# Attention, then two quantised convolutions: one projection of both pairs of heads per image, and fifteen images of the first convolution in DRAM

## The chip, the cores and the metric

The kernel runs on one core of a Trainium2 chip. The metric is the device time of one execution in microseconds; the median of the runs is quoted. An engine is named by the short names of the profile: PE is TensorE, DVE is VectorE, ACT is ScalarE, POOL is GpSimd, SP is SyncE (which only issues DMAs here).

## The reference

Two layers on x of shape (16, 128, 32, 32) in fp32: 16 images, 128 channels, N = 32 x 32 = 1024 positions. The first is self-attention with 4 heads of 128 channels each, an output projection and a residual. The second is two 3x3 convolutions with activations and weights quantised to 4 bits, a batch norm over all 16 images after each, and a residual.

```python
def _L0_conv_ref(x, w_qkv, b_qkv, w_out, b_out):
    qkv = jnp.einsum('bchw,oc->bohw', x, w_qkv) + b_qkv[None, :, None, None]
    ...
    scores = jnp.einsum('bnc,bcm->bnm', q, k) * c ** (-0.5)
    attn = jax.nn.softmax(scores, axis=-1)
    out = jnp.einsum('bnm,bmc->bnc', attn, v)
    ...
    out = jnp.einsum('bchw,oc->bohw', out, w_out) + b_out[None, :, None, None]
    return out + x

def _L1_conv_ref(x, w1, w2, gamma1, beta1, gamma2, beta2):
    identity = x
    out = act_quant(x)
    out = conv3x3(out, weight_quant(w1))
    out = batchnorm(out, gamma1, beta1)
    out = act_quant(out)
    out = conv3x3(out, weight_quant(w2))
    out = batchnorm(out, gamma2, beta2)
    return out + identity
```

The batch norm is the seam of the program: no image can be quantised for the second convolution before the first convolution of the last image is done.

## The kernel before, in words

The weights are folded first, so that the scores of a head are x times u with u = A x (tiles `psu`, `u`), and the values of every head are x itself; the output matrix B of a head holds both its value and its output weights.

**The attention, 63 of 64 heads in one pattern.** A head is 4 steps (NK = 4). A step computes four score tiles of 128 keys by 512 queries (`scores`, tiles `pss`, in three PSUM banks), turns each into exponentials on ACT (L585), and lets DVE form sums and differences of them (`mix`, L570 to L574). Half a step later `attend` (L597) multiplies them with the values by a Strassen-like scheme: a 2x2 block product in seven products and not eight, in four PSUM banks `psa` a0 to a3. TensorE is used as two independent halves of 64 columns, called lanes here (`LANES`, TOP and BOTTOM in the output's partitions); each product goes to one lane. Seven is odd, so one lane has one product more than the other in a step; `attend` alternates which.

At a head's end `evacuate` (L622) copies the four banks to SBUF on ACT, `combine` (L631) decodes them, `sum_up` and `normalise` (L698) divide by the sums of the exponentials. Two heads make a pair: `normalise` writes the two halves of head h into `z`, a tile of 7 blocks, and after the second head `mix` fills in the other three blocks of the scheme.

**The output projection.** `project_out` (L738) multiplies `z` of a pair with `wb_sb` by the same scheme, one PSUM bank after the other, all in the single bank `ps_m` ("mm") which `project_u` uses too. It is called for both pairs of an image, so there are 8 such banks per image. After each bank, ACT copies it out (L760 to L773). `gather_out` (L775) adds the pieces; the second pair's result is added to the first's in `accs[b]`, then bias and residual, and it is stored to `x1d`. The last image uses `project_plain` (L720) for its heads 0 and 1, and a separate tail (L873 writes its last sums).

**What sets the order.** On TensorE `product` (L400) ties every matmul behind the one issued before it. Everything else of the attention is placed by hand: `at(step, half, fn)` (L1018 on) puts a function behind the scores (half 0) or behind the products (half 1) of a step. Within that, the order on ACT, DVE, POOL and SP comes from the scheduler of the framework and from explicit `issue_after`; each engine then takes its instructions in that order.

**The two convolutions.** The first convolution of image b runs between the later heads' steps (tiles `psw`). Its output y stays in SBUF for images 0, 1 and 15; for `AWAY = range(2, B - 1)`, images 2 to 14, it goes to `y1d` in DRAM. After the last image, `bn_params(0)` gives scale and bias (L339), three loads bring `back` in groups of 2, 3 and 8 images (L1172 to L1174), `res` loads the residuals (L1179), and the second convolution runs image by image (L1238 to L1252): `quantize2` (L1181: ACT at L1189 from `y` or `back`, DVE at L1190 and L1194 into a padded tile), then nine taps (`conv`, tiles `psc`), or for `FILTERED` = 3, 5, 7, 9, 11, 13 a cheaper scheme (`filtered_conv`, L1209, tiles `psf`) with input rows from DVE and POOL (L1205) and four combinations on DVE (L1226 to L1229). DVE takes statistics at L298 (L292 for image 15), `gather` at L272 sums them, and after the second `bn_params` the last loop (L1255) writes the outputs.

Of the kernel before, what the change touches and what calls it, by code (L numbers as in the profile page):

```python
# [9 lines left out]
F32 = mybir.dt.float32  # L10
BF16 = mybir.dt.bfloat16
AF = mybir.ActivationFunctionType
ALU = mybir.AluOpType
# [3 lines left out]
NH = 4  # L17
# [176 lines left out]
def fast_path(  # L194
# [17 lines left out]
    P = 128  # L212
# [29 lines left out]
    AWAY = range(2, B - 1)  # L242
# [125 lines left out]
    with ExitStack() as ph:  # L368
# [5 lines left out]
        zp = pool("z", 1)  # L374
# [7 lines left out]
        accp = pool("acc", 2)  # L382
# [239 lines left out]
        def evacuate(g):  # L622
            evs[g] = [evp.tile([P, HALF], F32, tag=f"s{i}", name=f"ev_{g}_{i}") for i in range(4)]
            for to, ps in zip(evs[g], psa.pop(g)):
                nc.scalar.copy(to, ps)  # L625
# [72 lines left out]
        def normalise(g):  # L698
# [11 lines left out]
            if h % 2 == 0:  # L710
                zs[b] = zp.tile([P, 7, HALF], F32, tag="z", name=f"z_{b}_{h}")
            z = zs[b]
            for m in range(NHF):
                nc.vector.tensor_tensor(  # L714
                    z[:, 2 * (h % 2) + 1 - m], av[:, ts(m, HALF)], rb[:, ts(m, HALF)], ALU.mult
                )
            if h % 2:
                mix(z)

        def project_plain(g, m):  # L720
# [3 lines left out]
            ps = ps_m.tile([P, HALF], F32, tag="mm", name=f"pso_{g}_{m}")  # L724
            halves(ps, lambda t: bt_sb[:, h, LANES[t]], av[:, ts(m, HALF)])
            if h == 0:
                if m == 0:
                    accs[b] = accp.tile([P, N], F32, tag="acc", name=f"acc_{b}")
                nc.scalar.copy(accs[b][:, ts(m, HALF)], ps)
            else:  # L730
                half = accs[b][:, ts(m, HALF)]
                own = pjp.tile([P, HALF], F32, tag=("sa", "sb")[m], name=f"own_{m}")
                nc.scalar.copy(own, ps)
                nc.vector.tensor_tensor(half, half, own, ALU.add)
# [3 lines left out]
        def project_out(b, pair, bank):  # L738


            z = zs[b]
            four = [
                [(0, A11, B11)],
                [(1, A22, T4), (0, A12, B21)],
                [(1, S2, T2), (0, S4, B22)],
                [(1, S1, T1)],
            ]
            four[3 * pair].append((1 - pair, S3, T3))
            ps = ps_m.tile([P, HALF], F32, tag="mm", name=f"pso_{b}_{pair}_{bank}")
            for t, weight, head in four[bank]:  # L750
                product(ps[LANES[t]], wb_sb[:, weight, pair], z[:, head])
            if (b, pair) not in pjs:
                names = ("sa", "sb", "s3", "sd", "y", "s2")
                pjs[b, pair] = [
                    pjp.tile([P, HALF], F32, tag=n, name=f"{n}_{b}_{pair}") for n in names
                ]
            sa, sb, s3, sd, y, s2 = pjs[b, pair]
            if bank == 0:
                if pair == 0:
                    nc.scalar.copy(sa, ps)  # L760
                    nc.scalar.copy(y[BOTTOM], ps[BOTTOM])
                else:
                    nc.scalar.copy(sa[TOP], ps[TOP])  # L763
# [5 lines left out]
            else:  # L769
                nc.scalar.copy(sd[BOTTOM], ps[BOTTOM])  # L770
                nc.scalar.copy(sd[TOP], ps[BOTTOM])
                if pair == 1:
                    nc.scalar.copy(y[BOTTOM], ps[TOP])  # L773

        def gather_out(b, pair, part):  # L775

            sa, sb, s3, sd, y, s2 = pjs[b, pair]
# [8 lines left out]
            else:  # L786
                pjs.pop((b, pair))
                for half, first, second in ((1, y, sd), (0, sa, sb)):
                    if pair == 0:
                        if half:  # L790
                            accs[b] = accp.tile([P, N], F32, tag="acc", name=f"acc_{b}")
                        to = accs[b][:, ts(half, HALF)]
                        nc.vector.tensor_tensor(to, first, second, ALU.add)
                    else:
                        to = accs[b][:, ts(half, HALF)]
                        nc.vector.tensor_tensor(first, first, second, ALU.add)
# [744 lines left out]
```

## Time and profile before

| what | value |
|---|---|
| median of 3 runs | 2015.97 us (2015.92 to 2017.56) |
| profiled execution | 2017.06 us |
| span in its profile | 2015.2 us |
| granted TensorE clock, mean | 0.993 |
| one image of the attention | 118.8 us |
| last `psa` matmul of the attention ends | 1918.07 us |
| batch norm 1's bias done (L339) | 1925.25 us |
| first matmul of the second convolution | 1926.51 us |
| last matmul | about 1982.6 us |

The span is what the profiler saw; the execution's own time has 1.86 us around it. A row of the page's group list has the line, engine and operation, the tiles written and read, the shape, the number of instructions, then busy time and mean duration, and last the idle time just before these instructions with what ended it. A row of the timeline has start, duration, engine, line, operation, tiles and count. Durations of matmuls overlap: one is 0.59 us long while the next has started, so a busy TensorE may still be late.

The shares by slice of the span show an even attention, and after it the hand-over and the second stage in the last two or three of the 40 slices:

```profile
PE   9999999999999999999999999999999999999993
...
DVE  5886879778687877868787786888878698786887
```

### The profile page before, as it was taken

How to read it: one execution, taken by the hardware profiler on the slowest of the kernel's cores; microseconds unless marked ns; L12 is line 12 of the kernel's file. 1: busy time of each engine (PE TensorE's matmuls, PEld its weight loads, DVE VectorE, ACT ScalarE, POOL GpSimd, SP SyncE). 2: the span in 40 equal slices, each digit the busy share in tenths (PEclk: the TensorE clock that was granted, in tenths of full speed). 3: DMA queues.
4: the chain of work that ended last, by engine and by line, in shares of the span. 5: the costliest groups of instructions: out<-in, count | busy, mean ns of one | idle time of the engine just before them, and what ended most of it. 6: DMA issues, size and time to landing. Idle time of an engine off the chain costs nothing. (4 is left out here: it accounts for less than half of the span.)

```text
span 2015.2 us, 26154 instructions
## 1 busy us (share of the span) xinstructions
PE 1978.1 (98%) x9636; PEld 1072.0 (53%) x9637; DVE 1605.5 (80%) x2793; ACT 1267.6 (63%) x2148; POOL 182.9 (9%) x218
## 2 busy tenths in 40 slices
PE   9999999999999999999999999999999999999993
PEld 4455465554646555464555546555554655556541
DVE  5886879778687877868787786888878698786887
ACT  4566666666656656765665666666666566666575
POOL 1100010010000000000101000000100100000020
PEclk9999999999999999999999999999999999999997
DMA  4334333333343343334333333433333333433174
GB/s 122 85 81 97 72 80 90 84 90 88 86 95 82 97 92 84 94 74 100 85 99 84 90 89 74 110 79 94 84 95 95 73 97 86 91 84 79 42 314 168
DMA packets 55672, 191.70 MB, mean 95 GB/s; under 512 B 6128, under 2 KB 6512, under 8 KB 55536
## 3 DMA queue, kind: packets, MB, share of 16 engines
q0 software_dynamic: 27216, 99.10, 26.1%
q1 hardware_dynamic: 25200, 81.08, 10.4%
q10 hardware_dynamic: 3120, 9.77, 1.6%
q8 instruction: 77, 1.26, 0.3%
q14 instruction: 59, 0.48, 0.1%
HBM read 34.22 MB, written 23.59 MB: 29 GB/s over the span
## 5 line engine op out<-in xcount | busy, mean ns | idle before, releaser
L403 PE MATMUL pss<-u,x 128*64 128x512 f32 (+1 forms) x4128 | 1045.1, 590 | 0.0
L403 PE MATMUL psa<-e,xt 128*64 128x512 f32 x3472 | 907.5, 592 | 0.0
L585 ACT ACTIVATE e<-pss 128x512 f32<-128x512 f32 x1008 | 589.6, 597 | 299.0 <-PE pss L403 293.4
L403 PEld LDWEIGHTS pss<-u,x 128*64 128x64 f32 x4128 | 474.4, 137 | 402.7 <-issue 225.6
L403 PEld LDWEIGHTS psa<-e,xt 128*64 128x64 f32 x3472 | 418.9, 137 | 335.8 <-issue 203.4
L571 DVE TENSOR_TENSOR e<-e 128x1024 f32<-128x1024 f32 x252 | 307.6, 1221 | 16.2 <-ACT e L585 11.6
L595 POOL DMA_DIRECT2D es<-e x189 | 163.3, 864 | 1690.8 <-DVE e L574 1391.2
L570 DVE TENSOR_TENSOR e<-e 128x512 f32<-128x512 f32 x252 | 171.2, 679 | 148.9 <-ACT e L585 148.5
L574 DVE TENSOR_TENSOR e<-e 128x512 f32<-128x512 f32 x252 | 173.3, 688 | 14.2 <-DVE e L571 0.5
L625 ACT COPY ev<-psa 128x512 f32<-128x512 f32 x252 | 137.1, 591 | 73.7 <-PE psa L403 72.0
L403 PE MATMUL psu<-x,at_sb 128*64 128x512 f32 x512 | 180.4, 592 | 0.0
L403 PE MATMUL pso<-z,wb_sb 128*64 128x512 f32 x420 | 166.2, 592 | 0.0
L714 DVE TENSOR_TENSOR z<-av,rb 128x512 f32<-128x512 f32 x120 | 78.5, 684 | 51.1 <-PE pso L403 51.1
L534 ACT ACTIVATE u<-psu,au_sb 128x512 f32<-128x512 f32 x127 | 87.4, 688 | 16.9 <-PE psu L403 15.0
L779 DVE TENSOR_TENSOR y<-sa,s 64x512 f32<-64x512 f32 x30 | 20.5, 684 | 92.1 <-ACT sa L763 46.7
L403 PEld LDWEIGHTS psu<-x,at_sb 128*64 128x64 f32 x512 | 65.5, 137 | 47.0 <-issue 22.8
L655 DVE TRANSPOSE_TENSOR_REDUCE part<-es 128x32 f32<-128x1024 f32 (+1 forms) x65 | 79.3, 1220 | 4.9 <-DMA es<-e 4.8
L695 DVE STREAM_TRANSPOSE rb<-sums 128x1024 f32<-128x1024 f32 (+1 forms) x66 | 79.8, 1209 | 1.6
L403 PEld LDWEIGHTS pso<-z,wb_sb 128*64 128x64 f32 x420 | 54.2, 137 | 45.0 <-issue 23.3
L645 ACT COPY ev<-y 64x512 f32<-64x512 f32 x63 | 38.8, 615 | 61.9 <-DVE y L643 61.9
L765 ACT COPY sb<-pso 128x512 f32<-128x512 f32 x30 | 17.6, 586 | 72.0 <-PE pso L403 72.0
L403 PE MATMUL psw<-rows,filters 128*64 128x256 bf16 x540 | 60.2, 278 | 0.0
(197 smaller groups left out, 1476.1 us busy)
## 6 DMA issues: line engine op xcount, KB each, us to landing
es<-e POOLq DMA_DIRECT2D x189, 512.0 KB, 4.5
es<-e SPq DMA_DIRECT2D x63, 512.0 KB, 2.9
xt<-in_xturned_dram SPq DMA_DIRECT2D x32, 256.0 KB, 3.4
x_dram<-acc SPq DMA_DIRECT2D x16, 512.0 KB, 4.5
x<-in_x_dram ACTq DMA_DIRECT2D x15, 512.0 KB, 4.8
res<-x_dram SPq DMA_DIRECT2D x1, 7680.0 KB, 35.7
y_dram<-y SPq DMA_DIRECT2D x13, 512.0 KB, 2.6
out_dram<-back SPq DMA_DIRECT2D x10, 512.0 KB, 3.1
```

What stands on the lines that cost most here:

```text
L403: done = nc.tensor.matmul(out_, lhsT=lhsT, rhs=rhs, start=start, stop=stop)
L534: copied = nc.scalar.activation(dst, ps, AF.Identity, bias=au_sb[:, h : h + 1])
L570: nc.vector.tensor_tensor(e[:, T3], e[:, B12], e[:, B22], ALU.add)
L571: nc.vector.tensor_tensor(e[:, T1 : T2 + 1 : T2 - T1], e[:, B12 : B11 + 1], e[:, B11 : T3 + 1 : T3 - B11], ALU.subtract)
L574: return nc.vector.tensor_tensor(e[:, T4], e[:, T2], e[:, B21], ALU.add)
L585: exps[:] = [nc.scalar.activation(e[:, 2 * c + 1 - m], ps, AF.Exp).ins]
L595: nc.gpsimd.dma_start(out=sides[g], in_=mine, accum_op=ALU.add)
L625: nc.scalar.copy(to, ps)
L645: nc.scalar.copy(sa[BOTTOM], y[BOTTOM])
L655: nc.vector.tensor_reduce(part, total.rearrange("p (k c) -> p k c", c=Q), AX.X, ALU.add, apply_transpose=True,)
L695: nc.vector.transpose(rb, rinv.unsqueeze(2).to_broadcast([P, n, Q]))
L714: nc.vector.tensor_tensor(z[:, 2 * (h % 2) + 1 - m], av[:, ts(m, HALF)], rb[:, ts(m, HALF)], ALU.mult)
```

## The change

- `project_out` is called once per image and bank, after head 3. For each of four banks both pairs' products go into the same bank: pair 0 starts the sum, pair 1 ends it. The seventh product (S3 times T3) of each pair is cut into two halves of 256 columns, one added into bank 0 on lane 1 (W1), one into bank 3 on lane 0 (W2). The matmuls are issued directly and not through `product`. Banks come in the order 2, 1, 3, 0.
- `gather_out` decodes once per image.
- `evacuate` copies banks 1 and 3; the new `evacuate_rest` copies banks 0 and 2 behind the first and the second exponential of the step after.
- `zs` is kept per pair, so pool `z` has two buffers; pool `acc` has one.
- `normalise` of heads 0 and 2 comes one step earlier, its multiplications behind the step's `mix`; the first `turned_differences` one step later.
- `project_plain` (last image): head 0's result goes into a tile `first`; head 1's first bank is a `ps_s` bank, and its two calls come half a step earlier each.
- `AWAY` is images 0 to 14: their y is stored to DRAM. `y1_dram` has 15 images, and the three loads hold images 0 to 1, 2 to 4, and 5 to 14.

```diff
--- before.py
+++ after.py
@@ -239,7 +239,7 @@
     for n in range(2):
         nc.gpsimd.memset(late[n][:, 0:1], float((B - 1) * N))
 
-    AWAY = range(2, B - 1)
+    AWAY = range(0, B - 1)
     ys = [None if b in AWAY else keep.tile([P, N], F32, name=f"y{b}") for b in range(B)]
     pads = []
     for i in range(NPAD):
@@ -371,7 +371,7 @@
         xp = pool("x", 2)
         up = pool("u", 2)
         xtp = pool("xt", 3)
-        zp = pool("z", 1)
+        zp = pool("z", 2)
         pjp = pool("pj", 1)
         ep = pool("e", 3)
         esp = pool("es", 2)
@@ -379,7 +379,7 @@
         evp = pool("ev", 1)
         smp = pool("small", 4)
         rbp = pool("rb", 1)
-        accp = pool("acc", 2)
+        accp = pool("acc", 1)
         stp = pool("stage", 1)
         ps_s = pool("ps_s", 3, space=PSUM)
         ps_a = pool("ps_a", 1, space=PSUM)
@@ -621,8 +621,14 @@
 
         def evacuate(g):
             evs[g] = [evp.tile([P, HALF], F32, tag=f"s{i}", name=f"ev_{g}_{i}") for i in range(4)]
-            for to, ps in zip(evs[g], psa.pop(g)):
-                nc.scalar.copy(to, ps)
+            for i in (1, 3):
+                nc.scalar.copy(evs[g][i], psa[g][i])
+
+        def evacuate_rest(g):
+            for n, i in enumerate((0, 2)):
+                with tc.issue_after(stepped[n]):
+                    nc.scalar.copy(evs[g][i], psa[g][i])
+            psa.pop(g)
 
 
 
@@ -708,59 +714,64 @@
                 nc.vector.scalar_tensor_tensor(accs[b], accs[b], bo2_sb, xt[b], ALU.add, ALU.add)
                 return
             if h % 2 == 0:
-                zs[b] = zp.tile([P, 7, HALF], F32, tag="z", name=f"z_{b}_{h}")
-            z = zs[b]
+                zs[b, h // 2] = zp.tile([P, 7, HALF], F32, tag="z", name=f"z_{b}_{h}")
+            z = zs[b, h // 2]
             for m in range(NHF):
-                nc.vector.tensor_tensor(
-                    z[:, 2 * (h % 2) + 1 - m], av[:, ts(m, HALF)], rb[:, ts(m, HALF)], ALU.mult
-                )
+                with nullcontext() if h % 2 else tc.issue_after(sums_added[0]):
+                    nc.vector.tensor_tensor(
+                        z[:, 2 * (h % 2) + 1 - m], av[:, ts(m, HALF)], rb[:, ts(m, HALF)], ALU.mult
+                    )
             if h % 2:
                 mix(z)
 
+        W0, W1, W2 = slice(0, HALF), slice(0, HALF // 2), slice(HALF // 2, HALF)
+
         def project_plain(g, m):
 
             b, h = heads[g]
             av = avs[g]
-            ps = ps_m.tile([P, HALF], F32, tag="mm", name=f"pso_{g}_{m}")
+            pool_, tag = (ps_s, "s") if (h, m) == (1, 0) else (ps_m, "mm")
+            ps = pool_.tile([P, HALF], F32, tag=tag, name=f"pso_{g}_{m}")
             halves(ps, lambda t: bt_sb[:, h, LANES[t]], av[:, ts(m, HALF)])
             if h == 0:
                 if m == 0:
+                    avs["first"] = stp.tile([P, N], F32, tag="y", name=f"first_{b}")
+                nc.scalar.copy(avs["first"][:, ts(m, HALF)], ps)
+            else:
+                if m == 0:
                     accs[b] = accp.tile([P, N], F32, tag="acc", name=f"acc_{b}")
-                nc.scalar.copy(accs[b][:, ts(m, HALF)], ps)
-            else:
-                half = accs[b][:, ts(m, HALF)]
                 own = pjp.tile([P, HALF], F32, tag=("sa", "sb")[m], name=f"own_{m}")
                 nc.scalar.copy(own, ps)
-                nc.vector.tensor_tensor(half, half, own, ALU.add)
+                nc.vector.tensor_tensor(accs[b][:, ts(m, HALF)], avs["first"][:, ts(m, HALF)], own, ALU.add)
             if m:
                 avs.pop(g)
 
-        def project_out(b, pair, bank):
-
-
-            z = zs[b]
+        def project_out(b, bank):
+
+
             four = [
-                [(0, A11, B11)],
-                [(1, A22, T4), (0, A12, B21)],
-                [(1, S2, T2), (0, S4, B22)],
-                [(1, S1, T1)],
+                [(0, A11, B11, W0), (1, S3, T3, W1)],
+                [(1, A22, T4, W0), (0, A12, B21, W0)],
+                [(1, S2, T2, W0), (0, S4, B22, W0)],
+                [(1, S1, T1, W0), (0, S3, T3, W2)],
             ]
-            four[3 * pair].append((1 - pair, S3, T3))
-            ps = ps_m.tile([P, HALF], F32, tag="mm", name=f"pso_{b}_{pair}_{bank}")
-            for t, weight, head in four[bank]:
-                product(ps[LANES[t]], wb_sb[:, weight, pair], z[:, head])
-            if (b, pair) not in pjs:
+            ps = ps_m.tile([P, HALF], F32, tag="mm", name=f"pso_{b}_{bank}")
+            for pair in range(2):
+                for t, weight, head, cut in four[bank]:
+                    nc.tensor.matmul(
+                        ps[LANES[t], cut],
+                        wb_sb[:, weight, pair],
+                        zs[b, pair][:, head, cut],
+                        start=(pair == 0),
+                        stop=(pair == 1),
+                    )
+            if b not in pjs:
                 names = ("sa", "sb", "s3", "sd", "y", "s2")
-                pjs[b, pair] = [
-                    pjp.tile([P, HALF], F32, tag=n, name=f"{n}_{b}_{pair}") for n in names
-                ]
-            sa, sb, s3, sd, y, s2 = pjs[b, pair]
+                pjs[b] = [pjp.tile([P, HALF], F32, tag=n, name=f"{n}_{b}") for n in names]
+            sa, sb, s3, sd, y, s2 = pjs[b]
             if bank == 0:
-                if pair == 0:
-                    nc.scalar.copy(sa, ps)
-                    nc.scalar.copy(y[BOTTOM], ps[BOTTOM])
-                else:
-                    nc.scalar.copy(sa[TOP], ps[TOP])
+                nc.scalar.copy(sa[TOP], ps[TOP])
+                nc.scalar.copy(y[BOTTOM, W1], ps[BOTTOM, W1])
             elif bank == 1:
                 nc.scalar.copy(sb, ps)
             elif bank == 2:
@@ -769,12 +780,11 @@
             else:
                 nc.scalar.copy(sd[BOTTOM], ps[BOTTOM])
                 nc.scalar.copy(sd[TOP], ps[BOTTOM])
-                if pair == 1:
-                    nc.scalar.copy(y[BOTTOM], ps[TOP])
-
-        def gather_out(b, pair, part):
-
-            sa, sb, s3, sd, y, s2 = pjs[b, pair]
+                nc.scalar.copy(y[BOTTOM, W2], ps[TOP, W2])
+
+        def gather_out(b, part):
+
+            sa, sb, s3, sd, y, s2 = pjs[b]
             if part == 0:
                 nc.vector.tensor_tensor(y[TOP], sa[TOP], s2[TOP], ALU.add)
             elif part == 1:
@@ -784,21 +794,12 @@
                 with tc.issue_after(stepped[3]):
                     nc.scalar.copy(sa[BOTTOM], y[BOTTOM])
             else:
-                pjs.pop((b, pair))
-                for half, first, second in ((1, y, sd), (0, sa, sb)):
-                    if pair == 0:
-                        if half:
-                            accs[b] = accp.tile([P, N], F32, tag="acc", name=f"acc_{b}")
-                        to = accs[b][:, ts(half, HALF)]
-                        nc.vector.tensor_tensor(to, first, second, ALU.add)
-                    else:
-                        to = accs[b][:, ts(half, HALF)]
-                        nc.vector.tensor_tensor(first, first, second, ALU.add)
-                        nc.vector.tensor_tensor(to, to, first, ALU.add)
-                if pair:
-                    nc.vector.scalar_tensor_tensor(accs[b], accs[b], bo2_sb, xt[b], ALU.add, ALU.add)
-                    nc.sync.dma_start(out=x1d[b], in_=accs[b])
-
+                pjs.pop(b)
+                acc = accs[b] = accp.tile([P, N], F32, tag="acc", name=f"acc_{b}")
+                nc.vector.tensor_tensor(acc[:, HALF:], y, sd, ALU.add)
+                nc.vector.tensor_tensor(acc[:, 0:HALF], sa, sb, ALU.add)
+                nc.vector.scalar_tensor_tensor(acc, acc, bo2_sb, xt[b], ALU.add, ALU.add)
+                nc.sync.dma_start(out=x1d[b], in_=acc)
 
 
         GROUPS = [(0, HALF), (HALF, 3 * N // 4), (3 * N // 4, N)]
@@ -1053,27 +1054,26 @@
             end = (g + 1) * NK
             at(end + 1, 0, sum_up, g)
             at(end, 1, evacuate, g)
+            at(end + 1, 0, evacuate_rest, g)
             at(end + 1, 0, combine, g, 0)
             at(end + 1, 1, combine, g, 1)
             at(end + 2, 0, combine, g, 2)
             if b < B - 1:
-                at(end + (3 if h % 2 else 5), 0, normalise, g)
+                at(end + 4 - h % 2, 0, normalise, g)
             elif g < LAST - 1:
                 at(end + 3, 0, normalise, g)
             else:
                 at(end + 2, 1, normalise, g)
             at(max(g * NK + 1, 2), 0, project_u, g + 1, 0)
             at(max(g * NK + 2, 3), 0, project_u, g + 1, 1)
-            if b < B - 1 and h % 2:
-                pair = h // 2
-                when = ((5, 1), (6, 1), (7, 0), (7, 1))
-                for (step, half), bank in zip(when, ((0, 2, 3, 1), (2, 0, 3, 1))[pair]):
-                    at(end + step, half, project_out, b, pair, bank)
-                at(end + 8, 0, gather_out, b, pair, 0)
-                at(end + 8, 0, gather_out, b, pair, 1)
-                at(end + 9, 0, gather_out, b, pair, 2)
+            if b < B - 1 and h == NH - 1:
+                for bank, (step, half) in ((2, (5, 1)), (1, (6, 1)), (3, (7, 0)), (0, (7, 1))):
+                    at(end + step, half, project_out, b, bank)
+                at(end + 8, 0, gather_out, b, 0)
+                at(end + 8, 0, gather_out, b, 1)
+                at(end + 9, 0, gather_out, b, 2)
             elif b == B - 1 and h < 2:
-                for m, (step, half) in enumerate((((4, 1), (5, 1)), ((5, 0), (5, 1)))[h]):
+                for m, (step, half) in enumerate((((4, 1), (5, 1)), ((4, 1), (5, 0)))[h]):
                     at(end + step, half, project_plain, g, m)
             if h == NH - 1:
                 at(end + 9, 1, lambda b: quantize(b, accs[b], A_LEVELS, 0.0), b)
@@ -1087,7 +1087,7 @@
                     at(end + 9, 1, load, b + 2, nc.scalar)
             if h == 2 and b + 1 < B:
                 at(end - 2, 0, load_turned, b + 1, 0)
-                at(end + 2, 1, turned_differences, b + 1, 0)
+                at(end + 3, 1, turned_differences, b + 1, 0)
                 at(end + 3, 0, load_turned, b + 1, 1)
                 at(end + 6, 1, turned_differences, b + 1, 1)
         for k, (step, half) in enumerate(((8, 0), (8, 1), (9, 1), (10, 1))):
@@ -1532,7 +1532,7 @@
             ).ap()
         )
     args.append(nc.dram_tensor("x1_dram", (b, c, h * w), F32, kind="Internal").ap())
-    args.append(nc.dram_tensor("y1_dram", (13, c, h * w), F32, kind="Internal").ap())
+    args.append(nc.dram_tensor("y1_dram", (15, c, h * w), F32, kind="Internal").ap())
     args.append(nc.dram_tensor("out_0_dram", (b, c, h * w), F32, kind="ExternalOutput").ap())
     with tile.TileContext(nc) as tc:
         attention_then_quantized_convs(tc, *args)
```

## The prediction

> **What bounds the kernel now.** I read the page first, then the stretches of the windows view, then the timeline at every place where TensorE is late, then the DMA and timeline views from 1915 us on.
>
> ```profile
> span 2015.2 us, 26154 instructions
> PE 1978.1 (98%) x9636; PEld 1072.0 (53%) x9637; DVE 1605.5 (80%) x2793; ACT 1267.6 (63%) x2148; POOL 182.9 (9%) x218
> L403 PE MATMUL pso<-z,wb_sb 128*64 128x512 f32 x420 | 166.2, 592 | 0.0
> L714 DVE TENSOR_TENSOR z<-av,rb 128x512 f32<-128x512 f32 x120 | 78.5, 684 | 51.1 <-PE pso L403 51.1
> ```
>
> TensorE is the bound: 98% busy, and no other engine above 80%. The pso row is the output projection: 420 instructions in 15 images, 28 per image. The 51.1 us in which DVE waits at L714 for pso is idle time of an engine that is not the bound, so removing it is worth nothing by itself. What counts is what TensorE does. The windows view says more, one line for one image period and two for the second stage (us, then busy and count of PE, PEld, DVE, ACT, POOL, clock, DMA share, GB/s):
>
> ```profile
> 300.00:418.80 118.80, 118.80 (x578) 65.24 (x576) 95.29 (x163) 75.77 (x131) 10.34 (x13) 1.00 0.37 85
> ...
> 1926.50:1941.00 14.50, 14.49 (x75) 7.27 (x76) 11.96 (x31) 10.71 (x16) 4.57 (x4) 1.00 1.02 415
> 1941.00:1982.30 41.30, 41.24 (x197) 18.84 (x194) 40.18 (x66) 29.68 (x37) 9.86 (x8) 1.00 0.43 175
> ```
>
> Through the attention TensorE has no idle time left that a busy column shows, and DVE 23.5 us per image. In the second stage TensorE is also never idle, but there DVE is nearly full too (40.18 of 41.30).
>
> A busy column hides small stalls, since a matmul's row lasts 0.59 us while the next starts. So I took the starts. The matmuls run in two 64-column halves ("lanes"), and in an undisturbed stretch each lane starts one 512-column fp32 instruction every 0.429 us, or 0.2145 us per instruction over both. What starts later than that is lost. Over the 15 images it is 13.4 us, 0.89 per image, in three places of 0.2 us (the scores pss behind late exponentials) and some 0.28 at the filter products psw. One of them in the timeline (start, duration):
>
> ```profile
> 539.99 3.39 PE L403 MATMUL pss<-u,x 128*64 128x512 f32 x13
> 540.41 0.59 ACT L765 COPY sb<-pso 128x512 f32<-128x512 f32 x1 [2.53 <-PE pso L403]
> ...
> 541.32 0.60 ACT L585 ACTIVATE e<-pss 128x512 f32<-128x512 f32 x1 [0.32 <-PE pss L403]
> ```
>
> The three are: (a) the step after bank 1 of pair 1 (here); (b) the step after bank 0 of pair 0, where L760 and L761 (465.98 to 467.16) stand ahead of exponential 0 (467.19); (c) the end of head 3 (490.2), where one lane is a product behind, because pair 0 gives its lone seventh product to one lane and pair 1 evens it out only later.
>
> **What the Trainium skill says.** "DMA: Bandwidth & Descriptors", section "Issuing engines are not separate DMA queues": all DMAs share the same 16 engines. The trace agrees: 1.02 share and 415 GB/s above, and loads land in the order of issue. "TensorE: Matmul & The Clock Gate", Part 1: after an idle window of some 3.4 us TensorE's clock is halved, and it takes a busy window to bring it back; the windows run free. The trace agrees: the last matmul ends at about 1982.6, the granted clock is 1.00 in 1984 to 1985, 0.65 in 1985 to 1986 and 0.50 in 1986 to 1988. "Perfetto Trace Analysis", section on the tensor engine's instructions: ACT and DVE are strict FIFOs. The trace agrees: exponential 0 above starts when the copy in front of it, begun at 540.41, is out of the way. The order that the program builds for them is therefore what decides below.
>
> **The change part by part.**
>
> Projection. Before, an image has 14 full products of two instructions each (28, as above). After, it has 12 full products and four of half width (W1 and W2 in both pairs): the same streamed columns in 32 instructions, so TensorE's 166.2 us stay. What goes is decoding, the copies of 4 of 8 banks and one round of additions per image on ACT and DVE; it stood beside TensorE, so by itself it gains nothing. The lanes are the gain: with W1 on one lane and W2 on the other, each image leaves both lanes even, so (c) should go: 0.21 x 15 = 3.2 us. (b) stays: bank 2's two copies now stand there. (a) stays and grows a little: sa (0.58) and the half-width y copy (estimated 0.35) stand where sb (0.59) stood, but these end earlier against exponential 0; I take +0.035 x 15 = 0.5. Attention -2.7; bounds -6 (part of b and psw go too, as ACT has less to do) and +3 (0.2 more per image).
>
> Evacuation of banks 0 and 2 after exponentials 0 and 1. The new order puts exponential 0 behind two evictions and two half copies, not four evictions. At 426.8 to 433 that gives: ev1 426.77, ev3, two copies, exponential 0 at about 428.6 (before 428.68), ev0 to 429.8, exponentials 1 and 2, ev2 to about 431.4. The next head's first product into bank 2 is due at 431.72 + 0.43 = 432.15. Margin 0.75 us: cost nothing.
>
> z with two buffers, accp with one, normalise moved, turned differences half a step later: DVE work hidden under 23.5 us of slack per image; nothing. The single acc must be stored before the next image's is written, 119 us later (store 4.5 us): nothing.
>
> Last image. TensorE stands still for 2.64 us while own is copied:
>
> ```profile
> 1898.58 1.08 PE L403 MATMUL pso<-av,bt_sb 128*64 128x512 f32 x4 [2.64 <-ACT own L733]
> 1917.84 0.42 DVE L873 TENSOR_TENSOR acc<-acc,rb 128x256 f32<-128x256 f32 x1
> ```
>
> The extra bank and `first` remove it. But DVE is busy from 1888.4 to 1907.1 without a gap and its chain ends the stage at L873; that hardly moves. I take -0.4, bounds 0 and -2.5.
>
> Images 0 and 1 in DRAM. Two more stores of 512 KB: nothing (DMA share 0.37). At the hand-over the three loads hold images 0, 1 / 2, 3, 4 / 5 to 14, the last 10 images and not 8:
>
> ```profile
> back<-y_dram SPq DMA_DIRECT2D x1, 4096.0 KB, 18.1
> back<-y_dram SPq DMA_DIRECT2D x1, 1536.0 KB, 8.7
> back<-y_dram SPq DMA_DIRECT2D x1, 1024.0 KB, 5.1
> ```
>
> The first was issued at 1918.22 and landed at 1923.28; the batch-norm bias it is used with is done at 1925.25. 2 us of cover: nothing. The second landed at 1929.48; image 3's first use was 1927.63, so ACT waits 1.85 us; image 2's pad is then ready at about 1933.4, needed at 1934.5: nothing, 0.2 taken. The third landed at 1939.41; two images more are 1.05 MB at 415 GB/s = 2.5 us, so about 1942. It now holds image 5, which was in the second. Image 5 is quantised ahead of image 4 on both FIFOs, so image 4 waits for it:
>
> ```profile
> 1934.91 0.95 DVE L1194 TENSOR_SCALAR pad<-steps 128x1024 bf16<-128x1024 bf16 x1
> 1941.07 2.15 PE L282 MATMUL psc<-pad,wq 128*128 128x512 bf16 x9
> 1942.21 0.69 DVE L1229 TENSOR_TENSOR back<-half,psf 128x512 f32<-128x512 f32 x1
> 1942.93 0.69 DVE L298 BATCH_NORM_STATS2 early<-back 128x6 f32<-128x512 f32 x1
> ```
>
> Before, pad 4 was written at 1934.91 and its convolution started at 1941.07. In the order that is built now, DVE does image 3's four combinations (to 1942.9) and two L298 (to 1944.3) first, then image 5: L1190, L1194, two L1205, then L1190 and L1194 of image 4: 0.42 + 0.43 + 0.78 + 0.42 + 0.43 less some overlap, 2.3 us. ACT's two L1189 (1.23 each from 1942) lie under it. Convolution 4 at about 1946.6: 5.5 us late, bounds 3.5 (if the load lands early and DVE takes the four combinations without waiting) and 8 (if the load is slowed). Behind it TensorE has 41.3 us of work and no gap, so the delay passes on. DVE is later by only 2.2 us, so it is no longer near the bound: at the end, L272 and three L292 (1.35 us) that ran after the last matmul (1982.6 to 1984.4) shrink to the last L292; -0.9 (0 to -1.2).
>
> Clock. TensorE idle for 5.4 us: at whatever phase, one of the skill's 3.4 us windows is at least 2.7 us idle; the one at the end of before held 0.7 us of work and the clock still fell. At half clock for the busy part of a window: 0.7 to 1.7 us, a second window in the worst case. I take +1.5, bounds 0 and 2.5.
>
> Sum: -2.7 - 0.4 + 0.2 + 5.5 - 0.9 + 1.5 = +3.2. The profiled execution took 2017.06 (span 2015.2 and 1.86 around it), 1.09 above the median 2015.97; on the profiled execution 2020.3, on the median, which I forecast, 2019.2.
>
> **Rivals.** Less than 0.2% (4.0 us) is what a measurement here can't tell from no change.
> 1. Faster: ACT and DVE, eased at the image's end, let nearly all score stalls go (9.7 of the 13.4 us), and the tail gives 2.5: -9.7 - 2.5 + 0.2 + 5.5 - 0.9 = -7.4, 2008.6. For it: all these stalls end at ACT. Against: (a) and (b) have a copy ahead of exponential 0 still.
> 2. Even: the delay is 4.0 and the clock holds: -2.7 - 0.4 + 4.2 - 0.9 = +0.2, 2016.2. For it: the load may land before 1942. Against: DVE's chain, not the load, sets 1946.6.
> 3. Slower: bank 2's eviction comes too late for the next head. Place: ev2 behind exponential 2 at every head's end; price 63 x 0.1 = 6.3 us for each 0.1 us of lateness; it decides when the copy ends over 0.75 us later than I have it, as when an L257 or psw copy slips in front. With 0.1: +9.5, 2025.5.
> 4. The decode isn't halved where it matters, or bank 2, twice as long, delays the scores: inside rival 3's time.
>
> **Numbers.** Forecast case 0.52 (own range 2016 to 2023), rival 1 0.13, rival 2 0.16, rivals 3 and 4 0.19. Range 2011.0 to 2026.0 leaves out the far part of rivals 1 and 3. Above 2020.0: 0.47 of the forecast case and all of rival 3, 0.44. Below 2011.9: rival 1 and a little, 0.15. Between: 0.41.
>
> **What would show it.** Right: a hole on TensorE ahead of psc of image 4 at about 1941 to 1946 with the clock at 0.5 after it; L1189 waiting for the third load until about 1942; no wait for own at 1896; the late starts per image down from 0.89 to about 0.7 us. Wrong: no hole, or psa waiting for L630's copies, or the stall at 490 still there.

## The result, and the profile after

| | before | after |
|---|---|---|
| median | 2016.49 us (2015.92 to 2019.0, 6 runs) | 2024.99 us (2024.47 to 2026.56, 6 runs) |
| span of the profiled execution | 2015.2 us | 2023.0 us |
| an ordinary image of the attention | 118.79 | 118.80 |
| last `psa` matmul ends | 1918.07 | 1919.08 |
| first convolution of the second stage starts | 1926.51 | 1927.59 |
| convolution 4 starts | 1941.07 | 1949.65 |
| last convolution matmul ends | 1982.24 | 1992.19 |
| from there to the end of the span | 32.93 | 30.83 |

The ratio is 1.0041, 95% interval 1.0028 to 1.0054: slower, by 8.5 us of the medians and 7.8 us of the spans. The table places it: +1.0 in the attention, +7.5 ahead of convolution 4 (8.6 less the 1.1 that was there already), +1.4 from convolution 4 to the last one, -2.1 behind it. Of the +1.0, 0.5 is there at the first score matmul (8.25 and 8.79 us). In the ten profiled executions of this document that one starts between 7.81 and 9.02 us, so this half isn't the change's.

The kernel before took 2017.68 us (median of 40 executions) beside experiments 1 to 4 and 2017.76 (8 executions) beside the others; the ratios given there are against these. Of the 40, 24 have a mean granted clock of 0.992 and spans of 2015.7 to 2018.9 us, the other 16 have 0.993 and 2014.3 to 2015.9, as the profiled one has (0.993, 2015.2); experiment 2 shows what may part them.

The page of the changed kernel, the lines that answer to those of before:

```profile
span 2023.0 us, 26071 instructions
...
PE 1978.9 (98%) x9697; PEld 967.3 (48%) x9697; DVE 1540.6 (76%) x2703; ACT 1179.7 (58%) x2028; POOL 182.6 (9%) x218
...
L761 PE MATMUL pso<-z,wb_sb 128*64 128x512 f32 (+1 forms) x480 | 134.6, 540 | 0.0
...
L721 DVE TENSOR_TENSOR z<-av,rb 128x512 f32<-128x512 f32 x120 | 78.2, 683 | 0.0
```

The change does what it says: DVE is busy 65 us less, ACT 88 us less, 32 instructions of pso per image, and DVE's 51.1 us of waiting at the multiplication into z are gone. None of it shortens the span. The pso row reads 134.6 where it read 166.2, with the same columns streamed. That is no saving: where rows of two lanes lie over each other, the busy column gives the time to one of them, and TensorE's total is 1978.9 against 1978.1.

The windows view of the changed kernel shows the hole (us, then busy and count of PE, PEld, DVE, ACT, POOL, granted clock, DMA share, GB/s):

```profile
1927.50:1942.00 14.50, 14.41 (x75) 7.14 (x75) 9.66 (x26) 7.94 (x12) 2.21 (x2) 1.00 1.02 413
1942.00:1949.60 7.60, 0.32 (x2) 0.00 (x0) 7.36 (x12) 4.64 (x4) 2.67 (x2) 0.74 1.02 422
...
1948.00:1949.00 1.00, 0.00 (x0) 0.00 (x0) 1.00 (x1) 0.00 (x0) 0.84 (x1) 0.50 0.98 406
...
1951.00:1952.00 1.00, 1.00 (x4) 0.35 (x3) 0.79 (x2) 1.00 (x2) 0.75 (x1) 0.50 1.07 442
1952.00:1953.00 1.00, 1.00 (x4) 0.34 (x3) 0.93 (x1) 1.00 (x2) 1.00 (x2) 0.76 0.99 410
1953.00:1954.00 1.00, 1.00 (x6) 0.49 (x5) 0.63 (x1) 1.00 (x3) 0.92 (x1) 1.00 1.05 434
```

TensorE works 0.32 of 7.60 us, while DVE is full (7.36). The clock falls in the hole (at 1945.66) and TensorE then works about three more microseconds, up to 1952.48, at half speed: 4 matmuls in a microsecond, afterwards 6 or 7.

The hole is 7.7 us from the last start of the filtered convolution 3 to the first of convolution 4; that is 7.5 more than in the kernel before, and 7.33 of it are idle. Why it is so long is in the timeline (start, duration):

```profile
1933.07 0.77 DVE L1205 TENSOR_TENSOR rows<-padf 128x544 bf16<-128x544 bf16 x2
...
1943.23 4.64 ACT L1189 ACTIVATE steps<-back,bias,scale 128x1024 bf16<-128x1024 f32 x4 [2.26 <-DVE half L1228]
1943.30 0.69 DVE L1229 TENSOR_TENSOR back<-half,psf 128x512 f32<-128x512 f32 x1
1944.02 1.29 DVE L298 BATCH_NORM_STATS2 early<-back 128x6 f32<-128x512 f32 x2
1945.22 0.41 DVE L1190 TENSOR_SCALAR steps<-steps 128x1024 bf16<-128x1024 bf16 x1
1945.67 0.43 DVE L1194 TENSOR_SCALAR padf<-steps 128x1024 bf16<-128x1024 bf16 x1
1946.13 1.73 DVE L1205 TENSOR_TENSOR rows<-padf 128x544 bf16<-128x544 bf16 x2
1946.18 2.67 POOL L1205 TENSOR_TENSOR rows<-padf 128x544 bf16<-128x544 bf16 x2 [7.11 <-DVE padf L1194]
1947.78 1.35 DVE L1190 TENSOR_SCALAR steps<-steps 128x1024 bf16<-128x1024 bf16 x1
1949.16 0.43 DVE L1194 TENSOR_SCALAR pad<-steps 128x1024 bf16<-128x1024 bf16 x1
...
1949.65 3.51 PE L282 MATMUL psc<-pad,wq 128*128 128x512 bf16 x9 [7.33 <-DVE pad L1194]
```

ACT starts image 5 at 1943.23; the third load (5120 KB, 20.9 us) landed at 1943.15. The view names L1228, which ended at the same moment (1943.19); in the run of experiment 1 the load landed at 1933.74 and ACT went on at 1933.82, half a microsecond after L1228, so it is the load. The load opens the hole, and DVE's queue sets its end: the first L1189 is done at 1944.47, but DVE takes it up only at 1945.22, behind image 3's combinations and the two L298. DVE's chain is the one forecast, but two of its members are long: the two L1205 take 1.73 us where two took 0.77 for image 3, and image 4's L1190 1.35 where it takes 0.41, both while POOL makes its own two rows.

**The attention.** Summing what starts later than the lanes' cadence, per image: before 0.89 us, after 0.90 us in an ordinary image. The same sum hides an exchange (the last column is the kernel of experiment 1, whose ordinary image takes 118.18 us).

| late start in an ordinary image | before | after | old evacuation |
|---|---|---|---|
| scores, places (a), (b), (c) | 0.21 + 0.19 + 0.21 | 0 | 0 |
| filter products psw | 0.28 | 0.14 | under 0.1 each |
| scores of head 0, two steps after the image's end | 0 | 0.55 | 0.12 |
| pso of bank 3, in head 1 | 0 | 0.21 | 0 to 0.11 |
| sum | 0.89 | 0.90 | 0.29 |

Image 10 has 1.97 and image 12 has 2.37 us after the change, 1.07 and 1.47 more than an ordinary one. In the last image the wait for own (3.02 us counted this way) is gone.

### The profile page after: what moved, and what is told of

The parts are those of the page before. It is cut to its first block, busy times and chain, and to the rows that moved or that the text cites. A ratio compares the mean times of both kernels' runs of the same rounds, so it can differ in the third digit from the quotient of the medians.

```text
span 2023.0 us, 26071 instructions
## 1 busy us (share of the span) xinstructions
PE 1978.9 (98%) x9697; PEld 967.3 (48%) x9697; DVE 1540.6 (76%) x2703; ACT 1179.7 (58%) x2028; POOL 182.6 (9%) x218
## 4 chain that ended last, share of the span: by engine, by line
PE 82%; DVE 12%; issue 3%; ACT 2%; DMA 1%; DVEq 0%; POOL 0%; ACTq 0%; POOLq 0%
PE pss L403 36%; PE psa L403 31%; PE pso L761 5%; PE psu L403 5%; DVE e L571 2%; PE psc L282 2%; PE psw L403 2%; DVE e L574 1%; ACT e L585 1%; DVE z L721 1%; DVE part L661 1%; DVE back L1267 1%; DVE e L570 1%; DVE side L689 1%; PE psf L1214 1%
## 5 line engine op out<-in xcount | busy, mean ns | idle before, releaser
L403 PE MATMUL psa<-e,xt 128*64 128x512 f32 x3472 | 897.5, 592 | 0.0
L403 PEld LDWEIGHTS pss<-u,x 128*64 128x64 f32 x4128 | 430.5, 137 | 458.3 <-issue 346.7
L403 PEld LDWEIGHTS psa<-e,xt 128*64 128x64 f32 x3472 | 375.8, 137 | 377.0 <-issue 302.0
L571 DVE TENSOR_TENSOR e<-e 128x1024 f32<-128x1024 f32 x252 | 307.5, 1220 | 18.8 <-ACT e L585 13.7
L761 PE MATMUL pso<-z,wb_sb 128*64 128x512 f32 (+1 forms) x480 | 134.6, 540 | 0.0
L625 ACT COPY ev<-psa 128x512 f32<-128x512 f32 x126 | 70.8, 587 | 67.3 <-PE psa L403 66.8
L661 DVE TRANSPOSE_TENSOR_REDUCE part<-es 128x32 f32<-128x1024 f32 (+1 forms) x65 | 79.3, 1220 | 8.3 <-DMA es<-e 8.3
L403 PEld LDWEIGHTS psu<-x,at_sb 128*64 128x64 f32 x512 | 58.7, 138 | 56.4 <-issue 48.6
L648 ACT COPY ev<-y 64x512 f32<-64x512 f32 x63 | 38.9, 617 | 79.3 <-DVE y L644 79.3
L630 ACT COPY ev<-psa 128x512 f32<-128x512 f32 x126 | 72.8, 579 | 0.3 <-PE psa L403 0.3
L651 ACT COPY ev<-y 64x512 f32<-64x512 f32 x63 | 38.8, 616 | 58.7 <-DVE y L649 58.4
L789 DVE TENSOR_TENSOR y<-sa,s 64x512 f32<-64x512 f32 x15 | 10.2, 683 | 66.7 <-ACT sa L773 66.7
## 6 DMA issues: line engine op xcount, KB each, us to landing
back<-y_dram SPq DMA_DIRECT2D x1, 5120.0 KB, 20.9
```

The source lines that it names most:

```text
L403: done = nc.tensor.matmul(out_, lhsT=lhsT, rhs=rhs, start=start, stop=stop)
L571: nc.vector.tensor_tensor(e[:, T1 : T2 + 1 : T2 - T1], e[:, B12 : B11 + 1], e[:, B11 : T3 + 1 : T3 - B11], ALU.subtract)
L630: nc.scalar.copy(evs[g][i], psa[g][i])
L661: nc.vector.tensor_reduce(part, total.rearrange("p (k c) -> p k c", c=Q), AX.X, ALU.add, apply_transpose=True,)
L761: nc.tensor.matmul(ps[LANES[t], cut], wb_sb[:, weight, pair], zs[b, pair][:, head, cut], start=(pair == 0), stop=(pair == 1),)
```

## The experiments

**1. The old evacuation.** The new late start at the scores of head 0 (0.50 us in one start, 0.55 with the next) has this in the timeline of the changed kernel:

```profile
491.63 1.22 DVE L571 TENSOR_TENSOR e<-e 128x1024 f32<-128x1024 f32 x1
492.77 0.68 DVE L644 TENSOR_TENSOR y<-ev,y 128x512 f32<-128x512 f32 x1
...
493.48 0.62 ACT L648 COPY ev<-y 64x512 f32<-64x512 f32 x1 [1.73 <-DVE y L644]
494.17 0.68 DVE L649 TENSOR_TENSOR y<-y,ev 128x512 f32<-128x512 f32 x1
494.88 0.61 ACT L651 COPY ev<-y 64x512 f32<-64x512 f32 x1 [0.78 <-DVE y L649]
495.52 1.57 ACT L585 ACTIVATE e<-pss 128x512 f32<-128x512 f32 x3
```

Decoding a head is a chain that goes to and fro: DVE L644, ACT L648, DVE L649, ACT L651. The last copy stands in ACT's queue ahead of exponential 0 of the next step, so the scores wait. In the trace of the changed kernel L644 starts within 2 us behind the start of an L571 (1.22 us) in 60 of 63 heads. In the kernel before, the same addition starts within 2 us ahead of L571 in 46 heads.

```diff
-            for i in (1, 3):
+            for i in (1, 3, 0, 2):
                 nc.scalar.copy(evs[g][i], psa[g][i])
+            psa.pop(g)
...
-            at(end + 1, 0, evacuate_rest, g)
```

The four copies stand together again, in the order 1, 3, 0, 2 (the kernel before has 0, 1, 2, 3).

> The changed kernel, but all four banks of a head are copied out together at (end, 1) as before. Theory A (the late copy of bank 2 puts DVE's first addition of the decoding behind the 1.22 us of L571, so that its last half copy on ACT comes late in front of the next step's exponential 0): the late start of 0.50 us in head 0 of every image goes, and with it the 1.0 and 1.4 us of two images; the span falls from 2023.0 by 7 to 11 us. Rival B (the moved normalise and turned differences fill DVE's queue there): the 0.50 us stay, the span within 2 us of 2023.0. Rival C (four copies in a row delay exponential 0 again): the 0.2 us stalls at the scores of before come back, span 2019 to 2022.

Span 2013.5, 9.5 us under the changed kernel; median 2015.37, ratio to the kernel before 0.9988, interval 0.9980 to 0.9997. The late start fell to 0.12 us, and nothing of (a), (b), (c) came back. The timeline of this run:

```profile
487.30 0.68 DVE L645 TENSOR_TENSOR y<-ev,y 128x512 f32<-128x512 f32 x1
487.74 0.59 ACT L585 ACTIVATE e<-pss 128x512 f32<-128x512 f32 x1
487.90 1.22 DVE L571 TENSOR_TENSOR e<-e 128x1024 f32<-128x1024 f32 x1
```

The addition (now L645) comes before L571, as it does in 59 of 63 heads. Theory A holds for the 0.50 us, and neither rival: the moved normalise is still in this kernel, and the stalls of before did not return. The expectation was wrong for images 10 and 12: they are still 1.20 and 1.00 us longer than an ordinary image of this run, where the changed kernel has 1.07 and 1.47, and image 14 is now 1.05 longer. So these have a cause of their own. Some 11 us before each of these late starts DVE waits for the sums' accumulating DMA (at L661 1.00 and 1.39 us in the changed kernel; 1.13, 0.92 and 0.97 in the three images here). The kernel before has neither these waits nor these late starts, so they came with another part of the change; which part was not tried.

**2. Images 0 and 1 in DRAM, and nothing else.**

```diff
-    AWAY = range(2, B - 1)
+    AWAY = range(0, B - 1)
...
-    args.append(nc.dram_tensor("y1_dram", (13, c, h * w), F32, kind="Internal").ap())
+    args.append(nc.dram_tensor("y1_dram", (15, c, h * w), F32, kind="Internal").ap())
```

> The kernel before with images 0 and 1 in DRAM as well, and nothing else of the change. If the hole in the second stage comes from the third load alone: attention as before, a hole of 7 to 8 us ahead of psc of image 4, half a clock after it, 2 us given back at the end: span 2015.2 + 6 to 7.5. If the hole needs the rest of the change (the later hand-over, other work on DVE): hole under 4 us, span under 2019.

```profile
1950.13 5.68 PE L282 MATMUL psc<-pad,wq 128*128 128x512 bf16 x18 [7.32 <-DVE pad L1194]
```

and in the windows view:

```profile
1899.00:1902.00 3.00, 3.00 (x14) 1.46 (x12) 3.00 (x5) 0.77 (x2) 0.00 (x0) 0.50 0.02 5
```

Span 2023.4, median 2025.36, ratio 1.0039 (1.0025 to 1.0054). The hole ahead of convolution 4 is the same 7.7 us. The span is 8.2 us over the kernel before, 0.7 more than the upper end of what was expected. 6.7 of the 8.2 come behind the attention, as after the change (6.8). The other 1.5 were not expected: the attention ends at 1919.57, 1.5 us later than before, though nothing in it was edited. Up to the last image this run is even 0.2 us ahead. Then TensorE waits 2.7 us for own, as it did before the change, and from 1898.73 on its clock is 0.50 for 3.41 us; in the trace of the kernel before the same wait left it at 1.00. So the loads alone account for nearly all that the whole change costs in these traces. The change removes that wait, and with it this loss where it occurs.

**3. Image 5 in a load of its own.**

```diff
-        for lo, hi in ((0, 2), (2, 5), (5, len(AWAY))):
+        for lo, hi in ((0, 2), (2, 5), (5, 6), (6, len(AWAY))):
```

> The changed kernel with four loads at the hand-over and not three: images 0 to 1, 2 to 4, 5 alone, 6 to 14. If the wait for image 5's load is the cause of the hole: it closes to under 1.5 us, the clock stays, the span falls by 5.5 to 7.5 us to about 2016.5. If DVE's queue makes the hole (image 5's work in front of image 4's, whenever the load lands): a hole of 3 us or more stays, and the span falls by less than 4.

```profile
1941.14 4.13 PE L282 MATMUL psc<-pad,wq 128*128 128x512 bf16 x18
```

Span 2016.2, 6.8 us less; median 2018.57, ratio to before 1.0004 (0.9995 to 1.0013). Convolution 4 starts at 1941.14, right behind the filtered convolution 3, and the clock holds. A smaller hole of 1.4 us follows, ahead of convolution 6. Image 6 is in the last load now, but that had landed at 1942.22; ACT took its first image at 1943.86, behind the copy of convolution 4's first half (L293). So the way the images are grouped into loads is what makes the hole. The edit does it in two ways that this run doesn't part: image 5 is there earlier, and with it the order that is built changes, so that DVE's work for images 5 and 4 stands ahead of the four combinations of image 3 and not behind them.

**4. Plain image before filtered image.**

```diff
-            if b + 4 in FILTERED:
-                quantize2(b + 4)
+            if b + 3 in FILTERED and b > 1:
+                quantize2(b + 3)
```

> The changed kernel with the three loads as they are, but each filtered image quantised behind the plain image before it (5 behind 4, 7 behind 6 and so on). If the order in the queues turns a late load into the hole: convolution 4 starts within 1 us of the end of the filtered convolution 3, a smaller hole of 1 to 4 us comes ahead of psf of image 5, and the span falls by 3 to 6 us. If the load alone sets it: the hole moves to image 5 with its whole size, the span falls by less than 2.

```profile
1948.32 2.75 PE L1214 MATMUL psf<-rows,middle 128*128 128x512 bf16 x6 [2.32 <-DVE rows L1205]
```

Span 2019.2, 3.8 us less; median 2020.62, ratio to before 1.0016 (1.0009 to 1.0023). Convolution 4 starts at 1941.87, without a gap; ahead of psf of image 5 there are 2.5 us. With the load as late as ever (1942.91), the hole is a third: the order in the queues turned a load late for image 5 into one late for image 4. Even what is left is not the load's alone: ACT takes image 5 at 1944.59, 1.7 us after the landing, behind a copy of convolution 4. The span gains less than the hole, because the clock still falls: it is 0.50 for 3.41 us from 1948.45 on, and the six matmuls above take 2.75 us where six took 1.48. (Image 4's work on DVE stands ahead of the four combinations here, as in experiment 3, and image 5's behind them.)

**5. All rows of image 5 on DVE.**

```diff
-                engine = nc.vector if k in (1, 2) else nc.gpsimd
+                engine = nc.vector if k in (1, 2) or b == 5 else nc.gpsimd
```

> The changed kernel with all four input rows of image 5 (L1205) made on DVE; POOL makes none for it. In the changed kernel DVE's two took 1.73 us and the next L1190 1.35 us while POOL made the other two. If DVE and POOL hold each other up: now DVE's four take 0.43 us each, L1190 0.4, and image 4's convolution starts 0.3 to 0.8 us earlier after the filtered convolution 3 although DVE has two more instructions in front of it. If DVE was slow for another reason (the running load, say): 0.87 us each, and convolution 4 starts 2 us later.

```profile
1946.02 1.50 DVE L1205 TENSOR_TENSOR rows<-padf 128x544 bf16<-128x544 bf16 x4
1947.43 0.76 DVE L1190 TENSOR_SCALAR steps<-steps 128x1024 bf16<-128x1024 bf16 x2
1948.10 0.42 DVE L1194 TENSOR_SCALAR pad<-steps 128x1024 bf16<-128x1024 bf16 x1
```

Span 2021.7 (one execution, as in experiments 6 and 7, so the stretches inside it are compared and no interval can be given). Four rows take 1.50 us where two took 1.73, and two L1190 take 0.76 where one took 1.35. From the start of the filtered convolution 3 to convolution 4 it is 9.18 us, 10.13 before this edit: 0.95 less, a little more than was expected, with two more instructions of L1205 and one more L1190 on DVE. The transfers went on as before (DMA share 1.03), so they are not the reason: DVE and POOL hold each other up. The Trainium skill says so ("SBUF — State Buffer", section "SBUF: two separate sides"): DVE, in instructions with two inputs in SBUF and in some of its modes, shares a pair of SBUF ports with POOL, and whoever has it has it for a whole instruction. The trace agrees. Taken one by one, the first of the two L1205 took 0.44 us in the changed kernel and the second 1.37, beside POOL's first row (1.38); L1190 took 1.35, beside POOL's second (1.32). That is the price here: 0.93 and 0.94 us for the one on DVE that waits, and 0.2 to 0.3 for POOL, whose rows for image 3 took 1.12 each. (L1190 has one input; that it runs in one of those modes is not shown.)

**6. TensorE kept busy in the hole.** 26 matmuls that nobody reads, behind the filtered convolution 3; nothing of the computation changes.

```diff
             if b in FILTERED:
                 filtered_conv(b)
+                if b == 3:
+                    idle = ps_c.tile([P, HALF], F32, tag="c", name="idle")
+                    flat = wq[0].rearrange("p t o -> p (t o)")
+                    for _ in range(26):
+                        nc.tensor.matmul(idle, lhsT=wq[1][:, 0, :], rhs=flat[:, 0:HALF], start=True, stop=True)
```

> The changed kernel with 26 matmuls of 512 columns (about 5.5 us) that nobody reads between the filtered convolution 3 and convolution 4: nothing of the computation changes. If the half clock after the hole costs time: granted clock 1.0 all through 1942 to 1956, the hole's end where it was, and the last matmul and the span 1.2 to 1.7 us earlier than in the changed kernel (2023.0). If DVE bounds what follows: the clock stays up and the span doesn't move.

```profile
1942.00:1948.90 6.90, 5.22 (x25) 2.14 (x22) 6.66 (x11) 4.64 (x4) 2.67 (x2) 1.00 1.02 421
1948.90:1953.00 4.10, 4.06 (x19) 1.83 (x20) 2.99 (x5) 3.69 (x4) 2.46 (x2) 1.00 1.03 422
```

The clock stays at 1.00. From convolution 4 to the last matmul it is 41.18 us, as before the change (41.17), where the changed kernel has 42.54. The half clock cost 1.36 us. The span is 2020.7, 2.3 us less. Of the rest, 0.7 was there when the attention ended: with the same attention, the runs of the changed kernel and of experiments 3 to 6 end it between 1918.06 and 1919.08. The last 0.3 came behind the last matmul. The four other traces with a hole of this kind (experiments 1, 2, 5 and 7) lost between 1.3 and 2.0 us in the same stretch.

**7. Banks 0 and 3 of the projection exchanged.**

```diff
-                for bank, (step, half) in ((2, (5, 1)), (1, (6, 1)), (3, (7, 0)), (0, (7, 1))):
+                for bank, (step, half) in ((2, (5, 1)), (1, (6, 1)), (0, (7, 0)), (3, (7, 1))):
```

> The changed kernel with banks 0 and 3 of the projection exchanged in time: bank 0 (lane 0 full, lane 1 half) at (7, 0), bank 3 at (7, 1). If the 0.21 us late start of pso in head 1 comes from bank 3's uneven lanes meeting the lane that is ahead: it goes, 15 x 0.21 = 3.1 us, span about 2020. If it is a wait for the single bank: it stays, or grows.

Span 2021.9. The 0.21 us of pso went in every image, but 0.16 us came at psw one head later; an ordinary image fell from 0.90 to 0.81, 1.3 us over all images and not 3.1. The span alone could not show so small a gain: 1.0 of its 1.1 us was there when the attention ended, within what runs of one attention differ by. The result agrees with the first theory in the place (in bank 3 one lane has two full products, the other two halves) and not in the size: most of what went came back one head later. That the lanes' imbalance is the cause is likely from this, and not shown.

**8. Old evacuation, and four loads.** The edit of experiment 1, and loads of images 0 to 1, 2 to 4, 5 to 7, 8 to 14:

```diff
-        for lo, hi in ((0, 2), (2, 5), (5, len(AWAY))):
+        for lo, hi in ((0, 2), (2, 5), (5, 8), (8, len(AWAY))):
```

> The changed kernel with all four banks of a head copied out together at (end, 1), as before, and four loads at the hand-over: images 0 to 1, 2 to 4, 5 to 7, 8 to 14. If the two causes add up: attention as in the run with the old evacuation (span 2013.5), and no hole: less 7.5, less 1.4 of clock, plus 2.1 at the end, so a span of about 2006.7 and a ratio to the kernel before of about 0.9955. If a new wait comes (image 5 or 8 too late): a hole of over 1 us ahead of psf or psc, span over 2009.

Span 2006.5; median 2007.85, ratio to the kernel before 0.9950, interval 0.9936 to 0.9964. It beats both kernels: 8.7 us of span under the one before, 16.5 under the changed one. The sum is nearly what was expected (2006.7), in part by chance: 0.45 us are left ahead of convolution 4, a new hole of 1.5 us came ahead of convolution 8, the first image of the last load, and against that the end behind the last matmul is 30.6 us and did not grow by the 2.1 that had been reckoned.

## Why the prediction came out as it did

The direction of the sum was right, +3.2 against +7.8 us of span; its terms were right and wrong as follows.

- **Attention, -2.7.** Wrong. (c) went, as forecast, and (a) and (b) went as well, against the forecast; but new late starts of the same sum came. When the last image reaches the place where it had waited for own, the attention is some 3.9 us behind (0.5 in the start, 0.6 in image 0, 2.3 in images 1 to 14, nearly all of it in images 10 and 12, and 0.5 in image 15's first head). The step that failed is "Evacuation of banks 0 and 2": cost nothing. It looked at TensorE's next need of bank 2, which indeed had its margin, and not at the next reader of the copy: DVE's addition, which falls behind a 1.22 us instruction, and from there back to ACT and the scores. Experiment 1 showed it: 9.5 us of span. Images 10 and 12 are not explained by it. The slower rival had the right place (bank 2's late copy at a head's end) and the wrong mechanism, as no psa waited.
- **Last image, -0.4.** Too small. The wait for own left and nearly the whole of it was gained, about 2.9 us: the attention's end is only 1.0 us later although it was 3.9 us behind. That DVE was full there up to 1907 did not bind the end.
- **First and second load: nothing.** Right: the second stage starts 8.5 us after the last psa in both, and the filtered convolution 3 some 11.9 us later in both.
- **Convolution 4, +5.5.** The mechanism was right (experiments 2, 3 and 4), its size 7.5. The order and the instructions were those named; the term "0.42 + 0.43 + 0.78 + 0.42 + 0.43" was mis-sized. POOL's rows beside DVE make it 0.95 + 0.94 us longer (1.73 for the 0.78 reckoned, 1.35 for 0.41), which experiment 5 took away in part. The trace of before had a sign of it: pad 4's L1194 took 0.95 us at 1934.91 beside POOL's rows.
- **Clock, +1.5.** Right: 1.36 (experiment 6). One reading behind it was off: the last matmul of the kernel before ends at 1982.24 and not at 1982.6, so the 3.4 us ahead of that fall held 0.35 us of work and not 0.7. How empty they must be is not known from this: in experiment 4 they held 1.09 us and the clock still fell.
- **End of the second stage, -0.9.** Right in kind, 2.1 in size: between the last matmul and the second bias there are 2.4 us where there were 4.25, as not only L292 but ACT's three copies (L293) had been late behind L272. (L272 itself began before the last matmul ended, at 1981.95.)
- **Decoding, z, acc, moved normalise: nothing.** Right as far as the runs show, with one open end: the late starts in images 10, 12 and 14 came with some part of the change, and none of these parts was tried alone. The halved seventh product seems to cost 0.21 us per image at pso (experiment 7), where I had priced the uneven lanes in bank 3 at nothing.

The faster rival, that the score stalls go, is what the attention does without the late evacuation: 0.29 us per image in experiment 1.

That the result lies in the stated range owes something to luck. The median of 2024.99 is 5.8 us over the forecast of 2019.2, beyond the 2016 to 2023 of the forecast case, in the part of the range that was there for rival 3. And the errors have both signs: leaving out the 0.5 of the start, the attention came out 6.1 us worse than reckoned up to the last image and convolution 4 2.0 worse, the last image 2.5 and the end 1.2 better.

## What to carry to other kernels

When a copy out of PSUM is put off, follow its value to the next two engines and read what stands in their queues between; a margin at the PSUM bank says only that TensorE doesn't wait. When tiles are grouped into loads, ask which tile of a group is used first and what is queued behind it: two images more in a load cost 2.8 us of transfer (20.9 for 18.1), and 7.5 us on TensorE, because an image not yet due waited in front of one that was. A chain of short DVE instructions should not be priced by their quiet durations where POOL works at the same time: here an instruction of 0.4 us waited out one of POOL's. And a smaller hole on TensorE isn't cheaper in proportion: a third of this one still brought half clock (experiment 4).

## What the runs showed of the hardware that was not expected

- A plain bf16 TENSOR_SCALAR of 128x1024 on DVE (L1190) took 1.35 us, not 0.41, beside a TENSOR_TENSOR of POOL.
- TensorE's two 64-column lanes may run out of step without loss (starts 0.06 and 0.37 us apart by turns, at 538 us of the changed kernel). With two full products for one lane and two halves for the other in one bank, 0.21 us were lost in every image, although the next bank evens them out. The exchange of the banks moved most of the loss and didn't remove it.
- The length of a hole alone does not say whether TensorE's clock falls. It fell after idle times of 2.3 us (experiment 4) and 2.7 us (experiment 2), for 3.41 us each time, and stayed at 1.00 after 2.6 us in the last image of the kernel before and after 1.3 us in experiment 3.
